# One period of a two-layer decoder's last stage, listed in another order

## The chip, the cores and the metric

The kernel runs on one core of one Trainium2 chip. A core has five engines that each work through a queue of their own, strictly in order: TensorE (PE, matrix products and transposes; its weight loads are shown apart as PEld), VectorE (DVE), ScalarE (ACT), GpSimd (POOL) and SyncE (SP), whose queue here only issues DMAs. Engines wait for one another by semaphores. SBUF is the working memory; PE writes into PSUM, from which ACT and DVE carry the results off.

The metric is the device time of one execution in microseconds (us), the median of several runs. Less is better.

## The reference, cut to what matters

A batch of 16 sequences of 256 tokens of width 128 goes through two layers of attention, cross-attention and a mixture of experts, all in f32. Only the last two steps of the second layer are touched here: a cross-attention whose keys and values come from 64 context rows per sequence (16 heads of 8), and a mixture of 8 experts of which each token uses the best 2.

```
x = x + _L1_xattn_ref(ctx_1024, _layernorm(x, axis=-1), ...)   # softmax over 64 context rows, 16 heads
x = x + _L1_ffn_ref(_layernorm(x, axis=-1), ...)               # router, top 2 of 8, plus a shared expert

# within _L1_ffn_ref
scores = jax.nn.softmax(xt @ gate_w, axis=-1)
top_w, top_i = jax.lax.top_k(scores, TOP_K)
h = jax.nn.silu(jnp.einsum('th,ehi->eti', xt, wg)) * jnp.einsum('th,ehi->eti', xt, wu)
moe = jnp.einsum('eth,te->th', jnp.einsum('eti,eih->eth', h, wd), cw)
```

## The kernel before, in words

The 4096 tokens are 8 chunks (c) of 512 tokens. A chunk has four tiles of 128 tokens (0 to 3) and holds two sequences (0 and 1, of two tiles each). The earlier stages, layer 0 and layer 1's attention, end about 1270 us into the execution; the rest is the stage that is changed. In it the work of one chunk is cut into some 105 parts, and the string PLAN (from L2086) lists all parts once, each with a lag. The program walks the list again and again with a counter c0, and a part with lag n does the work of chunk c0 - n: `fl:1` belongs to the chunk before c0, `S0:-1` to the one after it. So one pass of the list holds the work of four or so chunks at different depths, and the chunks flow through as in a pipeline. The parts are issued under a manual schedule: PE, DVE, ACT and POOL each get their instructions in exactly the order of the list. Parts of chunks 0 and 1 that layer 1's attention already did (`begun`, L1472) are left out.

The parts, by engine (a digit is a tile, a sequence or an expert pair):

- **PE**: S scores of a tile (L1829), T transposes of half a tile's softmax (L1889), P transposes of the softmax's reciprocal sums (L1876), V values (L1907), Y output projection (L1923), xt and xq transposed input and queries (L1440, L1452), ft and fl transposed mixture input and router logits (L1945, L1954), fw the routing weights transposed (L1989), h gate and up products of two experts or of the shared one (L2017, h0 is the shared), d down products of a tile (L2035).
- **DVE**: G row maxima of S (L1836), B scores less maxima (L1840), R sums and reciprocals (L1862, L1863), O and X evacuate V and Y (L1915, L1929), xs and fs statistics (L1422, L1423), fg the router's choice of two experts, twelve small instructions after a copy of fl's result (L1961, L160 to L178), fq its weights (L1972 to L1982), m gate times up (L2024), z the final sum (L2044), D a half tile's transposes carried off (L1898).
- **ACT**: E exponentials (L1848), C the same work as D (L1898), U, xc, xQ, fc and fW carry off P, xt, xq, ft and fw, fn normalises (L1936), fe one exponential for the router (L1966), a the gate's silu (L2021). Exponential and silu come from different tables, so ACT loads a table (ACT_TABLE_LOAD, at the line of the instruction that needs it) whenever the two alternate.
- **POOL**: A two additions that shrink a softmax to a quarter (L1854, L1855), Q spreads R (L1868), K keys (L1464), xb a bias, xr and fr inverse square roots, k multiplies an expert pair by its routing weights (L2030).
- **SP**: fW also writes the routing weights to memory and reads them back spread over all partitions (wrows L1996, spread L2001, 512 KB), for the k parts; z sends two finished tiles to the output (L2051).

Memory that couples the engines: `sx`, one PSUM tile that S writes and G and B read, so that S, G, B take turns; two PSUM buffers ("m") that all of V, xq, Y, T, P, ft, fl, d, xt and fw share in turn, so that each waits for the carrying-off of the one two before it; and one PSUM buffer each for gate and up.

## Time and profile before

| | |
|---|---|
| Median of 3 runs | 1544.63 us (1543.79 to 1545.28) |
| The profiled execution's own time | 1540.27 us |
| Its span, first to last instruction | 1538.6 us |
| Busy over the span | PE 95%, DVE 76%, ACT 63%, POOL 43% |
| The stage that is changed | about 1266 us to the end, 272 us |
| Mean granted TensorE clock over the span | 0.982 |

How to read the views: a page gives busy shares over the whole span, which averages stages with different limits. So the stage has to be read from the timelines of each engine, in which a row is: start in us, duration in us (for a group of several instructions, from the first start to the last end), engine, line, operation, result and operands, shape, count, and in brackets the idle time of the engine before it with the engine and line that ended that idle time. In the table of windows, a row is a stretch, its length, then busy time and number of instructions on PE, PEld, DVE, ACT and POOL, the granted TensorE clock (1.00 is full), the DMA engines' mean busy share and GB/s.

### The profile page before, as it was taken

What the parts mean: (1) busy time and instruction counts of PE and PEld (TensorE: products, weight loads), DVE (VectorE), ACT (ScalarE), POOL (GpSimd) and SP (SyncE); (2) the same over time, 40 slices, a digit from 0 to 9 for tenths busy, and PEclk for the clock granted to TensorE, in tenths of its full rate; (3) what the DMA queues carried; (4) which work ended last, traced back from release to release, by engine and by line L of the source; (5) the groups of instructions that cost most, each with busy time, mean ns of one, the idle gap of its engine ahead of it and who ended that gap; (6) DMA issues with size and microseconds to landing.
All of it is one profiled execution on the core that took longest, in us unless ns stands there. A gap on an engine that the chain in (4) does not pass through costs nothing.

```text
span 1538.6 us, 34876 instructions
## 1 busy us (share of the span) xinstructions
PE 1461.4 (95%) x11569; PEld 1069.0 (69%) x11569; DVE 1175.6 (76%) x4620; ACT 971.1 (63%) x2619; POOL 667.9 (43%) x1102
## 2 busy tenths in 40 slices
PE   7999999999999999899999899999999996899897
PEld 4666666666666666689999777777777764565564
DVE  6666666667676767677878779999999978888863
ACT  5666565656565656354333368888888884767752
POOL 7354646464747464555533311101101015657643
PEclk9999999999999999999999989999999997999999
DMA  7760000000000000457777300000000000122122
GB/s 220 249 202 1 1 14 3 9 8 5 12 1 15 1 15 1 133 172 235 224 237 236 100 22 9 15 15 9 15 1 2 2 1 1 29 53 53 36 62 49
DMA packets 76321, 95.01 MB, mean 62 GB/s; under 512 B 15936, under 2 KB 59200, under 8 KB 76144
## 3 DMA queue, kind: packets, MB, share of 16 engines
q1 hardware_dynamic: 61312, 45.59, 10.9%
q10 hardware_dynamic: 10512, 38.28, 7.7%
q0 software_dynamic: 4320, 8.92, 1.7%
q8 instruction: 94, 1.54, 0.4%
q14 instruction: 83, 0.68, 0.1%
HBM read 64.11 MB, written 28.65 MB: 60 GB/s over the span
## 4 chain that ended last, share of the span: by engine, by line
PE 81%; DVE 12%; ACT 3%; issue 2%; DMA 1%; POOL 0%; POOLq 0%; ACTq 0%; SPq 0%; DVEq 0%
PE t L1659 7%; PE pqk L395 7%; PE s L450 6%; PE o L512 6%; PE t L497 5%; PE s L1627 5%; PE g L1298 4%; PE o L1674 4%; PE y L427 4%; PE y L1316 4%; PE u L1298 4%; PE pv L412 3%; PE pqk L1540 3%; PE yf L2035 2%; PE tx L1889 2%
## 5 line engine op out<-in xcount | busy, mean ns | idle before, releaser
L475 ACT ACTIVATE p<-p,nm 128x128 f32<-128x128 f32 (+1 forms) x512 | 227.5, 446 | 183.9 <-DVE nm L463 174.9
L486 POOL TENSOR_SCALAR p<-p,rs 128x128 f32<-128x128 f32 (+1 forms) x512 | 213.7, 434 | 187.3 <-DVE rs L484 159.4
L1649 ACT ACTIVATE p<-p,nm 128x256 f32<-128x256 f32 x512 | 225.7, 508 | 37.5 <-DVE nm L1638 35.2
L502 DVE COPY pT<-t 128x384 f32<-128x384 f32 x256 | 131.0, 553 | 102.4 <-PE t L497 102.3
L1638 DVE CUSTOM_DVE_ANT_0 p<-s,strip 128x256 f32<-128x256 f32 x512 | 188.1, 419 | 18.3 <-PE s L1627 17.8
L463 DVE CUSTOM_DVE_ANT_0 p<-s,strip 128x128 f32<-128x128 f32 (+1 forms) x512 | 158.1, 346 | 1.3 <-PE s L450 1.3
L1659 PEld LDWEIGHTS t<-ident,p 128*128 128x128 f32 x1024 | 111.2, 142 | 47.4 <-issue 12.6
L1659 PE MATMUL t<-ident,p 128*128 128x128 f32 x1024 | 141.5, 282 | 0.0
L1326 POOL DMA_INDIRECT rows_out<-yr,to x71 | 68.7, 967 | 117.3 <-DVE yr L1325 109.2
L1505 POOL TENSOR_SCALAR ve_a<-mv_a 128x2 f32<-128x2 f32 x16 | 3.7, 231 | 265.0 <-DVE mv_a L1500 264.9
L450 PE MATMUL s<-k,q 64*128 64x128 f32 (+1 forms) x1024 | 118.5, 350 | 0.0
L512 PE MATMUL o<-pT,v 128*64 128x256 f32 (+1 forms) x1024 | 112.8, 340 | 0.8 <-DVE pT L502 0.8
L497 PE MATMUL t<-ident,p 128*128 128x128 f32 x768 | 113.3, 283 | 0.2 <-ACT k L406 0.2
L450 PEld LDWEIGHTS s<-k,q 64*128 64x128 f32 x1024 | 67.0, 186 | 62.5 <-issue 56.3
L512 PEld LDWEIGHTS o<-pT,v 128*64 128x64 f32 x1024 | 62.9, 136 | 61.6 <-issue 25.9
L497 PEld LDWEIGHTS t<-ident,p 128*128 128x128 f32 x768 | 82.1, 141 | 23.2 <-issue 15.4
L475 ACT ACTIVATION_READ_ACCUMULATOR p<-p,nm 128x1 f32 x512 | 96.5, 188 | 0.0
L1306 ACT ACTIVATE gs<-gs 128x512 f32<-128x512 f32 x71 | 44.7, 630 | 77.0 <-DVE gs L1305 64.9
L1667 DVE COPY pT<-t 128x512 f32<-128x512 f32 x128 | 88.1, 688 | 6.2 <-PE t L1659 3.2
L1627 PE MATMUL s<-k,q 32*128 32x256 f32 x1024 | 85.3, 408 | 0.6 <-DVE nm L1638 0.5
L421 DVE COPY v<-pv 128x512 f32<-128x512 f32 x64 | 44.0, 687 | 50.8 <-PE pv L412 50.8
L790 POOL DMA_INDIRECT rows_in<-xn,slot_in x64 | 64.2, 1004 | 33.8 <-DVE nm L463 20.5
(338 smaller groups left out, 3487.8 us busy)
## 6 DMA issues: line engine op xcount, KB each, us to landing
gu<-in_L_ffn_gate_up_w ACTq DMA_DIRECT2D x71, 512.0 KB
rows_in<-zero SPq DMA_DIRECT2D x131, 130.0 KB
spread<-wrows SPq DMA_DIRECT2D x16, 512.0 KB
xr<-rows_in SPq DMA_DIRECT2D x71, 65.0 KB
y<-rows_out SPq DMA_DIRECT2D x16, 256.0 KB
x<-in_x SPq DMA_DIRECT2D x8, 256.0 KB
out_x<-yo SPq DMA_DIRECT2D x16, 128.0 KB
rows_out<-yr,to POOLq DMA_INDIRECT x71, 3.7
```

The source lines that it names most:

```text
L450: nc.tensor.matmul(ps_of[b, h][:, cols], q[rows, u2, iq], k[rows, u2, 0:nk], start=True, stop=True,)
L463: nc.vector.tensor_tensor_reduce(out=pr[:, cols], in0=ps[:, cols], in1=strip[:, h, P : 2 * P] if it == 0 else strip[:, h, :], scale=1.0, s ...
L475: nc.scalar.activation(pr[:, cols], pr[:, cols], AF.Exp, bias=nm[:, it : it + 1], scale=-1.0, accum_out=sm[:, it : it + 1],)
L486: nc.gpsimd.tensor_scalar(pr[:, cols], pr[:, cols], rs[:, it : it + 1], 1.0, ALU.mult, ALU.mult)
L497: nc.tensor.transpose(ps[:, cols], pr[:, cols], ident)
L502: nc.vector.tensor_copy(pT_of[b, h], tp_of.pop((b, h)))
L512: nc.tensor.matmul(po[rows, c0:N], v[:, jt, h % 8 * DH : (h % 8 + 1) * DH], pT[:, 0:N] if jt == 0 else pT[:, N:], start=(jt == 0), stop=(j ...
L1298: nc.tensor.matmul(ps[:, f, :], gu[:, lo + f * P : lo + (f + 1) * P], xT, start=True, stop=True,)
L1627: nc.tensor.matmul(ps_of[b, h][:, it, :], q[rows, g, it * P : (it + 1) * P], k[rows, g, :], start=True, stop=True,)
L1638: nc.vector.tensor_tensor_reduce(out=pr[:, it, :], in0=ps[:, it, :], in1=strip1[:, h, (1 - it) * P : (1 - it) * P + N], scale=1.0, scalar= ...
L1649: nc.scalar.activation(pr[:, it, :], pr[:, it, :], AF.Exp, bias=nm[:, it : it + 1], scale=-1.0)
L1659: nc.tensor.transpose(ps[:, jt, it * P : (it + 1) * P], pr[:, it, jt * P : (jt + 1) * P], ident,)
```

## The change

Only the string PLAN is replaced. The same functions are called for the same chunks, with two exceptions: the part D30 (DVE) becomes C30 (ACT), and the lags are numbered anew since the list now begins at another part. The lists hold 105 parts each.

```
         PLAN = (
-            "h3:2 Q1:0 a3:2 T21:0 B3:0 T11:0 K1:-1 m3:2 R2:0 xs0:-2 C21:0 S0:-1 T10:0 xr:-1 "
-            "C11:0 h4:2 P0:0 k1:2 k2:2 C10:0 V0:0 G0:-1 B0:-1 fn:1 a4:2 U0:0 ft:1 m4:2 fc:1 "
-            "O0:0 xs1:-2 E3:0 S1:-1 k3:2 Y0:0 G1:-1 fl:1 h0:1 k4:2 X0:0 d0:2 fg:1 T20:0 z0:2 "
-            "E0:-1 B1:-1 d3:2 C20:0 fs0:0 z3:2 d2:2 xt:-2 S2:-1 A3:0 fe:1 a0:1 fq:1 z2:2 "
-            "Q2:0 A0:-1 R3:0 Q3:0 fw:1 xc:-2 G2:-1 d1:2 z1:2 m0:1 fW:1 E1:-1 T31:0 K0:-3 "
-            "C31:0 T30:0 h1:1 P1:0 B2:-1 E2:-1 U1:0 S3:-1 A1:-1 D30:0 a1:1 V1:0 R0:-1 A2:-1 "
-            "xq:-2 xb:-2 G3:-1 O1:0 xQ:-2 m1:1 Y1:0 h2:1 a2:1 T00:-1 R1:-1 C00:-1 X1:0 fs1:0 "
-            "T01:-1 fr:0 Q0:-1 C01:-1 m2:1 "
+            "A0:0 a1:2 fs0:1 V1:1 z1:3 O1:1 xq:-1 xs0:-1 S3:0 K0:-2 R0:0 Y1:1 m1:2 xQ:-1 X1:1 "
+            "T21:0 fs1:1 C21:0 A1:0 h2:2 T10:0 G3:0 Q0:0 a2:2 xb:-1 m2:2 T11:0 fr:1 C10:0 h3:2 "
+            "T00:0 C11:0 T01:0 B3:0 k2:2 a3:2 C00:0 S0:-1 R1:0 m3:2 k1:2 xr:-1 xs1:-2 C01:0 "
+            "T20:0 fn:1 G0:-1 C20:0 Q1:0 A2:0 h4:2 a4:2 k3:2 B0:-1 m4:2 P0:0 V0:0 U0:0 O0:0 "
+            "k4:2 ft:1 S1:-1 Y0:0 fc:1 fl:1 R2:0 h0:1 G1:-1 a0:1 X0:0 Q2:0 d3:2 fg:1 z3:2 E3:0 "
+            "T30:0 fe:1 B1:-1 A3:0 C30:0 d0:2 E0:-1 xt:-2 m0:1 z0:2 S2:-1 fq:1 xc:-2 R3:0 Q3:0 "
+            "T31:0 d2:2 C31:0 fw:1 G2:-1 z2:2 h1:1 E1:-1 P1:0 K1:-2 fW:1 U1:0 d1:2 B2:-1 E2:-1 "
         )
```

For one period the queues then read as follows, from the router's logits on.

| Queue | Before | After |
|---|---|---|
| PE | fl h0 d0 T20 d3 d2 xt S2 fw d1 T31 T30 h1 P1 S3 V1 xq Y1 h2 ... | fl h0 d3 T30 d0 xt S2 T31 d2 fw h1 P1 d1 V1 xq S3 Y1 T21 h2 ... |
| DVE | G1 X0 fg z0 B1 fs0 z3 fq z2 ... | R2 G1 X0 fg z3 B1 m0 z0 fq R3 G2 z2 B2 ... |
| ACT | fc E3 E0 C20 fe a0 xc fW E1 C31 E2 U1 a1 ... | fc a0 E3 fe C30 E0 xc C31 E1 fW U1 E2 a1 ... |
| POOL | k3 k4 A3 Q2 A0 Q3 K0 A1 A2 ... | Q1 A2 k3 k4 Q2 A3 Q3 K1 A0 K0 A1 ... |
| SP | output of z2 and z3, wrows, output of z1 and z0, spread | output of z2 and z3, wrows, spread, output of z1 and z0 |

## The prediction

> **What bounds the stage now.** First the table of windows over the stage: five periods, from the h2 part of the first chunk to that of the sixth, take 147.38 us (29.5 each), and PE is busy in all but 11.4 of them. Then PE's own waits in that stretch: 10.7 of the 11.4 us have one cause.

> ```profile
> 1327.12:1474.50 147.38, 135.93 (x945) 89.18 (x944) 128.53 (x317) 102.99 (x154) 97.08 (x123) 0.98 0.19 45
> ...
> PE yf L2035 <- DVE yo L2044: 10.7, 5, 2.6
> ```

> Once a period PE waits until DVE has carried off a down product. PE's timeline of one period shows where, and DVE's and POOL's show why.

> ```profile
> 1398.00 0.96 PE L1954 MATMUL lg<-rw,xTf 128*128 128x8 f32 x8
> 1398.81 1.10 PE L2017 MATMUL g<-xTf,sg 128*128 128x512 f32 x2
> ...
> 1401.73 0.60 PE L1889 MATMUL tx<-ident,px 128*128 128x128 f32 x4
> 1404.14 0.49 PE L2035 MATMUL yf<-sd,hb 128*128 128x128 f32 x2 [1.82 <-DVE yo L2044]
> ```
> ```profile
> 1400.24 1.12 DVE L169 TENSOR_TENSOR eq_f<-eq_f,mi_f 128x32 f32<-128x32 f32 x1
> ...
> 1402.85 0.97 DVE L169 TENSOR_TENSOR eq_f<-eq_f,mi_f 128x32 f32<-128x32 f32 x1
> ...
> 1508.76 0.19 DVE L169 TENSOR_TENSOR eq_f<-eq_f,mi_f 128x32 f32<-128x32 f32 x1
> ```
> ```profile
> 1400.04 1.28 POOL L1854 TENSOR_TENSOR half<-px 128x512 f32<-128x512 f32 x1 [1.40 <-ACT px L1848]
> ...
> 1402.51 1.25 POOL L1854 TENSOR_TENSOR half<-px 128x512 f32<-128x512 f32 x1
> ```

> PE issues fl at 1398.00, then h0, d0, T20, and stands before d3, whose PSUM buffer is d0's and is free only after z0; on DVE z0 stands behind fg. fg runs 1399.13 to 1403.81, 4.7 us. Two of its instructions take 1.12 and 0.97 us: each has both inputs in SBUF and ends when POOL's addition (A3, then A0) does. In the drain, with POOL idle, the same instruction takes 0.19 and fg 2.7 us (1507.64 to 1510.36). So 2.0 us of fg is waiting for POOL; in other periods (1428 to 1433) it is 2.7.

> The gap has a second price. In one-microsecond windows the granted clock falls to half after the gap of 1373 (2.59 us) and after that of 1462 (1.82 us), and not after the other three.

> ```profile
> 1374.00:1375.00 1.00, 1.00 (x5) 1.00 (x6) 1.00 (x2) 1.00 (x1) 0.00 (x0) 0.50 0.00 0
> ...
> 1404.00:1405.00 1.00, 0.86 (x7) 0.86 (x8) 1.00 (x2) 0.98 (x2) 0.58 (x1) 1.00 0.00 0
> ```

> About 3.4 us run at half clock each time, which costs 1.7. A period with neither extra (V1 at 1384.28 to V1 at 1412.93) takes 28.65, of which 26.8 is PE's work and small waits.

> **The change, part by part.** No instruction is added or removed but for two table loads and D30; the sum is about places.

> *Removed: the router's collision.* POOL after: A2, k3, k4, Q2, then A3 only after E3. I walk one new period on all four queues, T=0 at fl's issue, with the durations of the rows (issue to issue on PE: S 0.65, T 0.44, h 1.72, h0 1.80, d 1.12, V 1.0, xq 0.95; G and B 1.14 each; E 1.05; A 2.04; k 1.24). G1 ends at 0.75, X0 at 1.1; fg starts there, as before (1.13 after fl). POOL has done A2 at -1.5, k3 at -0.3 and k4 at 0.95, before fg's first two-input instruction at 1.5. So fg takes 2.7 and ends at 3.85, z3 at 4.1. Before, z0 ended 6.1 after fl. If POOL is late by a microsecond, k4 delays fg by under one, which the next wait hides.

> *Added: a wait for E3.* Its place in ACT's queue is now behind a0. a0 needs h0's gate (0.81+1.10=1.91) and ends at 2.55; the table load follows it.

> ```profile
> 1397.52 1.28 ACT L1848 ACT_TABLE_LOAD   x1
> 1398.81 2.19 ACT L1848 ACTIVATE px<-px,rstd_x 128x1024 f32<-128x1024 f32 x2
> ```

> The exponential starts 1.29 after the load does: E3 runs 3.85 to 5.0. T30 transposes E3's result and stands on PE before d0, so PE, done with d3 at 3.89, waits to 5.05: **1.16 us, in place of 1.82 to 2.6**. Queued behind T30: d0, xt, S2, T31, d2, fw, h1. Behind E3 on ACT: fe, C30, E0, xc; fe at 5.0 is still ahead of fq, which now stands behind z0 (7.0).

> [...]

> *Further round the period.* d0 5.5, xt 6.6, S2 7.15 (B1 done 5.3), T31 7.8, d2 8.25, fw 9.4 (fq done 8.2), h1 9.8, P1 11.5, d1 11.85 (fW has freed the buffer at 10.6), V1 12.95, xq 13.95, S3 14.9 (B2 done 11.2), Y1 15.55, T21 16.0, h2 16.4. The silu load stands behind E2, so a1 comes only at 14.5 to 15.1 and m1 at 16.3; h2 needs a1 at 16.4 and m1 at 17.3: held. Then T10, T11 18.15, h3 19.05, T00, T01 20.75, S0 21.65 (B3 done 20.3), T20, h4 22.75, P0 24.45, V0 24.8, ft 25.8, S1, Y0, and fl at 27.55. With the odd tenths that PE loses at PSUM turns in the old period (0.35) that is 27.9; the other way, 28.65-1.82+1.16, is 28.0. ACT loses two of its four loads a period (-2.57) and gains C30 (+0.48); DVE loses D30 (-0.60): neither sets the end, so nothing is counted.

> *Moved past queues.* On SP, z1's output now comes after the spread instead of before it: neutral. The spread itself loses cover. k2 wants it at 19.45, where before k1 came 14 us after the weights were ready. The chain that ended last shows its length when POOL waited for it:

> ```profile
> 1514.21 1.46 DMA wrows<-cTf
> 1516.36 6.83 DMA spread<-wrows
> 1523.35 1.26 POOL hb L2030
> ```

> From the copy's end (1514.19) to k1 is 9.15 us. After fW at 10.6 that gives 19.75. k2, k1, xr and Q1 follow in POOL's queue (4.2 us), so P0 can start at 24.0; PE asks at 24.45. A2 behind Q1 ends at 26.0, R2 wants it at 26.15. Cover left: 0.2 to 0.45 us. I count 0.

> *The sum.* Five periods: 147.4 - 10.7 + 5 x 1.16 = 142.5. Of the half-clock stretches (2 x 1.7) I take half back, the trace showing no gap as short as 1.16 to judge by: 140.8, so -6.6. [...] Before the first of these periods: the turns of S, G and B through `sx` (3.8 each at 1275 to 1300) are as many in both orders; fg of the first chunk loses its 1.4 of collision (1311.56 to 1315.78 is 4.2), and half of its half-clock stretch (1319 to 1323) is 0.8: -2. The next-to-last period (25.10) loses its waits on z and gains E3's: -0.4. The drain is one chain, router, spread, weighting, down, in both: -0.2. In all **-9.2**: span 1538.6 to 1529.4, its own time 1540.27 to 1531.1. The median of the runs shown lies 4.36 above that execution; the same difference gives **1535.5**.

> **The rivals.** Less than 0.2% (3.1 us) either way is what a measurement of this kernel can't tell from no change.

> - *As summed* (-5 to -14, that is 1531 to 1540): 0.55. Its range holds the clock going either way and 0.5 us per period of waits unseen.
> - *The gap closes*: E3 is let through early enough or PE's other parts fill it. Then 5 x 1.16 more and no half clock at all: -17, 1528. For it: ACT has 2 us a period more room. Against it: the order of a0, load, E3, T30 is fixed. 0.07.
> - [...] 0.15, half of it beyond 3.1.
> - *The change does nothing to the wait*: POOL is so late in every period that k3 and k4 fall into fg as A3 and A0 did. Then z3 ends at 6.1 and the gap is the old one: 1545. 0.08.
> - *Slower: the spread lands late.* Place: k2, with k1, xr, Q1, A2 behind it in POOL's queue, P0 on PE behind Q1, fg behind R2. Six periods, each microsecond of landing past 0.45 of cover adds one to each. The gain of 9.2 is eaten from 9.15+0.45+1.5 = 11.1 us after fW on; at 12 it is 5 slower, 1550. For it: the cover falls from 14 us to 9, and outputs share the queue. Against it: in four periods DMA traffic after fW ends 8 us later, each time within half a microsecond. 0.15.

> Range: 1527 to 1547 leaves out the far half of the last and little else, some 0.13. Faster: 0.55+0.07+0.08=0.70 and 0.03 of the last case; same: 0.07+0.06+0.02; slower the rest, 0.12; I round to 0.73, 0.13, 0.14.

> **What would show it.** Right: PE's wait for yo L2044 in the stage falls from five gaps of about 2 us to none or under 0.3; a new wait of PE tx L1889 on ACT px L1848 of 1.0 to 1.3 us once a period; ACT_TABLE_LOAD twice a period, one at L1848 and one at L2021; L169 at 0.19 to 0.4 in the middle periods; h2 starts 27.7 to 28.3 apart. Wrong: POOL hb L2030 waiting on spread in more than the last chunk; PE rt L1876 waiting on POOL rs; half-clock windows after gaps of 1.2; a wait of PE for DVE's m parts, which the walk gives 0.1 to 1 us of room.

## The result, and the profile after

The new list takes 1530.89 us (median of 6 runs, 1529.08 to 1532.58) where the kernel before, over 6 runs, takes 1544.87 (1543.68 to 1545.68): 0.991 of it, 95% interval 0.9898 to 0.9923, or 14.0 us less. The two profiled executions lie 10.4 us apart (1540.27 and 1529.89). Predicted were 9.2 us for the execution and 1535.5 for the median, with 1531 to 1540 as the case "as summed": the median lies at its lower edge.

The table of windows of the new kernel, from the h2 of the first chunk to that of the second, and from there to that of the seventh (columns as in the row of before: length, then busy time on PE, PEld, DVE, ACT and POOL, the granted clock, the DMA engines' share and GB/s):

```profile
1325.42:1354.13 28.71, 26.99 (x192) 17.47 (x191) 23.30 (x65) 18.56 (x30) 18.97 (x26) 1.00 0.22 54
1354.13:1489.35 135.22, 128.46 (x905) 84.34 (x903) 106.46 (x296) 87.68 (x143) 89.03 (x112) 1.00 0.20 48
```

By the starts of h2 the periods are 28.71, 27.96, 27.95, 27.96, 26.50 and 24.85. The first five, which took 147.5 us before, take 139.1: 8.5 us less, at full clock throughout. PE's waits over the stage (in all, times, longest), and then POOL's:

```profile
PE tx L1889 <- ACT px L1848: 9.3, 7, 2.3
```
```profile
POOL hb L2030 <- DMA spread<-wrows: 16.0, 3, 14.9
```

PE's waits for yo L2044, 10.7 us before, are gone, and in their place stands T30's wait for E3's px. POOL waits for the spread routing weights 14.9 us in the last chunk, and 1.1 us in two others together.

One period of the new kernel by engine: PE, then DVE, ACT and POOL (start, duration, line, operation, and in brackets the idle time before it and what ended it).

```profile
1393.31 0.96 PE L1954 MATMUL lg<-rw,xTf 128*128 128x8 f32 x8
...
1396.15 1.06 PE L2035 MATMUL yf<-wd,hb 128*128 128x128 f32 x8
1398.38 0.66 PE L1889 MATMUL tx<-ident,px 128*128 128x128 f32 x4 [1.18 <-ACT px L1848]
```
```profile
1395.48 0.19 DVE L169 TENSOR_TENSOR eq_f<-eq_f,mi_f 128x32 f32<-128x32 f32 x1
...
1396.83 0.19 DVE L169 TENSOR_TENSOR eq_f<-eq_f,mi_f 128x32 f32<-128x32 f32 x1
...
1397.24 0.29 DVE L2044 TENSOR_TENSOR yo<-x,yf 128x128 f32<-128x128 f32 x1
```
```profile
1395.27 0.60 ACT L2021 ACTIVATE gs<-g 128x512 f32<-128x512 f32 x1 [2.46 <-PE g L2017]
1395.88 1.28 ACT L1848 ACT_TABLE_LOAD   x1
1397.18 1.15 ACT L1848 ACTIVATE px<-px,rstd_x 128x1024 f32<-128x1024 f32 x1
```
```profile
1398.40 1.28 POOL L1854 TENSOR_TENSOR half<-px 128x512 f32<-128x512 f32 x1 [3.99 <-ACT px L1848]
```

POOL idles 4 us before A3, so the two-input instructions of the router's choice take 0.19 us in place of about 1; fg takes 2.7, z3 starts 3.9 us after fl. PE then waits 1.18 us for E3, which comes straight behind a0 and a table load of 1.28. Over the stage ACT loads tables 17 times, not 27.

**Where the 10.5 us of the span came from**, by the starts of h2 in both traces: 0.8 are there already when the stage begins, 0.8 come before the first h2, 8.5 in the five periods, 0.25 in the next one and 0.25 in the drain.

### The profile page after: what moved, and what is told of

The parts are those of the page before. It is cut to its first block, busy times and chain, and to the rows that moved or that the text cites. A ratio compares the mean times of both kernels' runs of the same rounds, so it can differ in the third digit from the quotient of the medians.

```text
span 1528.1 us, 34888 instructions
## 1 busy us (share of the span) xinstructions
PE 1457.1 (95%) x11569; PEld 1065.8 (70%) x11569; DVE 1160.5 (76%) x4612; ACT 961.2 (63%) x2617; POOL 665.6 (44%) x1102
## 3 DMA queue, kind: packets, MB, share of 16 engines
HBM read 64.11 MB, written 28.65 MB: 61 GB/s over the span
## 4 chain that ended last, share of the span: by engine, by line
PE 82%; DVE 10%; ACT 3%; issue 2%; POOL 2%; DMA 1%; POOLq 0%; SPq 0%; ACTq 0%; DVEq 0%
PE t L1659 7%; PE pqk L395 7%; PE s L450 6%; PE o L512 6%; PE t L497 6%; PE s L1627 5%; PE g L1298 4%; PE o L1674 4%; PE y L427 4%; PE y L1316 4%; PE u L1298 4%; PE pv L412 3%; PE pqk L1540 3%; PE g L2017 2%; PE yf L2035 2%; DVE p L1638 2%
## 5 line engine op out<-in xcount | busy, mean ns | idle before, releaser
L486 POOL TENSOR_SCALAR p<-p,rs 128x128 f32<-128x128 f32 (+1 forms) x512 | 212.3, 431 | 188.1 <-DVE rs L484 160.1
```

The costliest lines, as they stand in the source:

```text
L486: nc.gpsimd.tensor_scalar(pr[:, cols], pr[:, cols], rs[:, it : it + 1], 1.0, ALU.mult, ALU.mult)
```

## The experiments

Twelve runs, one of them the new list again (e5), were meant to tell four things apart: whether the collision with POOL was the cost, what of POOL's work does it, what the idle time of PE costs beyond itself, and whether the 1.18 us that remain can be had. The first four ran on one chip and the next four on another, where both kernels take some 20 us longer, nearly all of it ahead of the stage (S0 starts at 1288.8 to 1291.5 us, not at 1265 to 1267); e10 to e12 ran on a third and e13 on a fourth. So a kernel is compared by its ratio to the kernel before on its own chip, and by the stage's length from the first S0 to the end of the span in its profile, which is 262.8 and 262.9 us for the new list on two chips.

| Kernel | Median, us | Before there | Ratio (95%) | Stage, us | Middle period, us | Half-clock stretches in the middle periods |
|---|---|---|---|---|---|---|
| before | 1544.87 | | 1 | 272.5 | 28.65 to 31.1 | 2 |
| new list | 1530.89 | 1544.87 | 0.991 (0.9898 to 0.9923) | 262.8 | 27.95 | 0 |
| e1_act_order | 1557.03 | 1565.67 | 0.9943 (0.9925 to 0.9962) | 264.8 | 28.07 | 0 |
| e2_collide | 1567.03 | 1565.67 | 0.9998 (0.9981 to 1.0016) | 280.7 | 30.7 | 4 |
| e3_gap | 1572.22 | 1565.67 | 1.0043 (1.0024 to 1.0062) | 280.0 | 30.7 | 5 |
| e4_d0_first | 1553.03 | 1565.67 | 0.991 (0.989 to 0.9931) | 260.5 | 27.74 | 0 |
| e5_after | 1553.61 | 1569.15 | 0.9908 (0.9892 to 0.9924) | 262.9 | 27.95 | 0 |
| e6_fill | 1555.06 | 1569.15 | 0.992 (0.9899 to 0.9941) | 263.3 | 27.95 | 0 |
| e7_half_gap | 1557.40 | 1569.15 | 0.993 (0.9911 to 0.9948) | 266.2 | 28.45 | 0 |
| e9_d0_z0 | 1551.13 | 1569.15 | 0.9891 (0.9872 to 0.9909) | 260.2 | 27.73 | 0 |
| e10_s2_first | 1530.25 | 1545.93 | 0.9908 (0.989 to 0.9926) | 260.4 | 27.64 | 0 |
| e11_split | 1550.81 | 1545.93 | 1.0043 (1.0026 to 1.0059) | 283.2 | 30.7 | 2 |
| e12_gap2 | 1544.41 | 1545.93 | 0.9991 (0.9982 to 1.0) | 276.0 | 28.8 or 30.35 | 4 |
| e13_split2 | 1535.53 | 1547.69 | 0.9924 (0.9901 to 0.9946) | 267.7 | 28.77 | 0 |

The middle period is from fl to fl; the stretches are counted from the first h2 on. Added operations write a tile that nothing reads. Two profiled executions are far from their medians: that of the kernel before took 4.4 to 4.6 us less, that of e2 took 6.2 us more.

### One part of the change alone: ACT's order

The old list with five ACT parts in another order: a0 goes first, as in the new list, and E0 last. The table loads fall from 27 to 17 with it.

```
 ACT behind fc
-E3 E0 C20 fe a0 ...
+a0 E3 C20 fe E0 ...
```

> The old list with five ACT parts in another order and nothing else: a0, E3, C20, fe, E0 after fc, where it was E3, E0, C20, fe, a0. Theory (the gain is the router's choice no longer meeting POOL's additions, since E3 and so A3 come later): fg takes 2.7 to 2.9 us in the middle periods, where it took 4.2 to 5.5; PE's wait for z0 falls from 1.8 to 2.6 to about 0.3; d2 waits 0.1 for C20 and fw about 0.4 for fq, which now touches A3's second addition. Net 1.2 us a period and the half-clock stretches gone: 8 to 14 us below the kernel before, 1531 to 1537. Rival (the gain lies in the other moves of the list: d3 ahead, T31 apart, V ahead of S3, D30 to ACT): at most 2 us below, 1543 to 1545.

Of the 9.7 us that the stage loses with the whole list, this part alone takes 7.7 in the profiles, and by the ratios (0.9943 and 0.991) some six tenths of the gain: with E3 behind a0, A3 and A0 come later, and fg is left alone. But the collision isn't gone, it has moved. DVE and PE of one period, and POOL's two additions:

```profile
1394.96 0.19 DVE L169 TENSOR_TENSOR eq_f<-eq_f,mi_f 128x32 f32<-128x32 f32 x1
...
1399.02 1.19 DVE L1982 TENSOR_TENSOR comb<-eq_f,eq_f 128x32 f32<-128x32 f32 x1
```
```profile
1400.47 0.60 PE L1989 MATMUL cT<-ident,comb 128*8 128x128 f32 x4 [1.11 <-DVE yo L2044]
```
```profile
1396.45 1.29 POOL L1854 TENSOR_TENSOR half<-px 128x512 f32<-128x512 f32 x1 [4.68 <-ACT px L1848]
...
1398.90 1.26 POOL L1854 TENSOR_TENSOR half<-px 128x512 f32<-128x512 f32 x1
```

Now fq's last instruction, which also has two inputs in SBUF, takes 1.19 us and ends within a tenth of a microsecond of A0, and fw (cT) waits 1.1 us. cT's PSUM buffer comes free with a yo, and that yo stands behind comb on DVE: it starts at 1400.14, and would have started about 1.0 earlier behind a comb of 0.19. The period is 28.07 with this gap in place of 27.95 with the other. The rest of the new order is worth the last 2 us of the stage in the profiles, about 5 by the ratios, give or take 3.

### Is it the collision, and what of POOL's work makes it?

The new list with work on POOL put back where the additions stood: three additions of 128x512 (e2), or seven fills of the same tile (e6), behind Q2.

```
+        pad = hbp.tile([P, 4, P], F32, tag="pad", name="pad", bufs=1)
+        def busy(c):
+            for _ in range(3):                                   # e2
+                nc.gpsimd.tensor_tensor(pad, ones.unsqueeze(1).to_broadcast([P, 4, P]),
+                    ones.unsqueeze(1).to_broadcast([P, 4, P]), ALU.add)
+            for _ in range(7): nc.gpsimd.memset(pad, 1.0)        # e6
-            ... X0:0 Q2:0 d3:2 fg:1 ...
+            ... X0:0 Q2:0 w:1 d3:2 fg:1 ...
```

> The new list with three additions of 128x512 on POOL (about 1.28 us each, into a tile that nothing reads) behind Q2, where POOL stands idle for 4 us until A3: they start with fg and are over before A3 can start. Theory (a DVE instruction with two inputs in SBUF stands while POOL's addition runs): fg grows from 2.7 to between 4.5 and 6 us, z3 ends at 6 to 7 us after fl's issue instead of 4.2, PE's d0, which ran at 5.5, waits for it by 0.5 to 1.5 us, so 4 to 12 us slower than the new kernel: 1535 to 1543. Rival (the gain has another cause, and POOL's idle time is free): no change from the new kernel, 1530 to 1532.

> The new list with seven fills of 128x512 on POOL behind Q2, into a tile that nothing reads: about as long as the three additions that gave back the whole gain (3.3 to 3.9 us, from 0.95 us for a fill of 128x1024), but instructions that read nothing. Theory (what holds up the router's instructions with two inputs in SBUF is POOL reading SBUF): fg stays 2.7 us, the gap before T30 stays 1.18, the time is that of the new list within 0.2%. Rival (POOL being busy, or being late with what follows, is enough): fg 4 us or more and a wait of PE for z3 or z0, 10 us or more above the new list.

POOL and DVE of one period with the additions, then with the fills:

```profile
1425.12 3.28 POOL L2094 TENSOR_TENSOR pad<-ones 128x512 f32<-128x512 f32 x3
...
1427.58 0.86 DVE L169 TENSOR_TENSOR eq_f<-eq_f,mi_f 128x32 f32<-128x32 f32 x1
...
1429.60 0.93 DVE L169 TENSOR_TENSOR eq_f<-eq_f,mi_f 128x32 f32<-128x32 f32 x1
```
```profile
1419.44 4.03 POOL L2094 MEMSET pad<- 128x512 f32 x7
...
1420.56 0.19 DVE L169 TENSOR_TENSOR eq_f<-eq_f,mi_f 128x32 f32<-128x32 f32 x1
...
1421.90 0.19 DVE L169 TENSOR_TENSOR eq_f<-eq_f,mi_f 128x32 f32<-128x32 f32 x1
```

The additions give back the whole gain (0.9998), some 14 us and not the 4 to 12 that were expected: fg takes 5.3 to 6.3 us from the second chunk on (its second long instruction above runs into A3, which starts at 1429.15), d0 waits 0.9 to 1.8 us for z3, on top of T30's 1.18, and four half-clock stretches follow. The fills are longer (4.03 us) and cover all of fg, and fg isn't touched; the time is within 0.1% of the new list's on that chip, and A3, a little late behind them, costs nothing. So POOL being busy or late was not the cause.

What is left is what the additions do and the fills don't, and that is to read SBUF; no run here parts this from other differences between the two. Two more things fit it. In the earlier layers of the kernel before, nb_f (L363, 128x4, two inputs in SBUF) takes 0.32 to 0.35 us and ends with POOL's operation in five of the six cases where it meets a multiplication of one tile by a column (L486); in the sixth, which falls between two of these, and in the two others it takes 0.15. And the hb product (L2024), whose second input is in PSUM, is not held up in the kernel before: it takes 0.69 us where it lies wholly beside POOL's k (seven of its 40 cases) and 0.67 to 0.69 in the others. In the rows of e2 and e6 the router's instruction with two inputs in SBUF takes 0.86 and 0.93 us beside additions, and 0.19 beside fills.

### What the idle time costs

The new list with ACT copies of 128x512 between a0 and E3, so that PE's one gap, before T30, grows: two copies (e3), one (e7), one and a copy of 128x128 (e12).

```
-            ... a0:1 X0:0 ... E3:0
+            ... a0:1 w:1 X0:0 ... E3:0      # w: 2, 1, or 1 and a quarter copies on ACT
```

> The new list with two copies of 128x512 on ACT (about 0.5 us each, into a tile that nothing reads) between a0 and E3: E3 ends 1.0 us later, and PE's gap before T30 grows from 1.18 to about 2.15 us, as long as the old kernel's gaps. Theory that a gap of this length sets off stretches of half clock: one to three of six middle gaps are followed by about 3.4 us at a granted clock of 0.50, 1.7 us each; 6.5 us for the gaps and 2 to 5 for the clock, 8 to 12 us slower than the new kernel: 1539 to 1543, mean granted clock down by 0.001 to 0.003. Rival (the half-clock stretches have nothing to do with the gap): 6 to 7 us slower, 1537 to 1538, clock as in the new kernel.

> The new list with one copy of 128x512 on ACT between a0 and E3 (two gave a gap of 2.32 us and 20 us more). Expected gap before T30: 1.18 + 0.57 = 1.75. If the granted clock only depends on the length of the idle time and 1.75 is still short enough: 0.57 us a period, 4 us above the new list. If 1.75 is enough to drop it after each gap, as 2.32 was: 0.57 + 1.6 a period, about 15 above. In between, as in the kernel before, where two gaps in five of 1.8 to 2.6 did it: 7 to 10 above.

> The new list with a copy of 128x512 and one of 128x128 on ACT between a0 and E3. Expected gap before T30: 1.18 + 0.57 + 0.25 = 2.0 us, just past the 1.8 of idle in one window of 3.41 us from which the clock seems to fall. Theory: a half-clock stretch follows where at least 1.82 us of the gap lie in one window, and none where the gap straddles two, which of the two is a matter of the phase: 2 to 5 stretches in the seven periods, 9 to 16 us above the new list. Rival (the length of the gap alone decides, with its limit between 1.75 and 2.32): all or none, about 6 or about 18 above.

The gaps came out at 2.32, 1.67 and 2.00 us, against 1.18 (2.15, 1.75 and 2.0 were expected). By its gap alone e3's period would grow by 1.14 us, and it grew by 2.75, because a stretch of 3.41 us at half clock follows each of the five middle gaps, where one to three were expected; the kernel lost some 20 us and not 8 to 12. With one copy the period grows by 0.50, the kernel by 3.8 us, and no stretch appears. What decides is not the length of the gap alone. The half-clock stretches of all the traces are whole multiples of 3.413 us (one cut off by the end of a trace aside) and, within a trace, begin on one grid of 3.413 (in the stage of the kernel before at 1319.30, 1373.91 and 1462.66 us, 16 and 26 times 3.413 apart). The table of windows, cut on that grid, first for the kernel with the gap of 2.00 us:

```profile
1374.07:1377.49 3.42, 1.42 (x13) 1.38 (x13) 2.02 (x3) 2.76 (x5) 1.28 (x1) 1.00 0.00 0
1377.49:1380.90 3.41, 3.41 (x20) 2.43 (x19) 2.37 (x10) 1.54 (x2) 1.45 (x3) 0.50 0.00 0
1404.79:1408.21 3.42, 1.75 (x16) 1.75 (x17) 1.73 (x2) 2.76 (x5) 1.65 (x2) 1.00 0.00 0
1408.21:1411.62 3.41, 3.41 (x32) 2.69 (x31) 3.21 (x12) 2.77 (x5) 1.74 (x4) 1.00 0.00 0
```

In the first row the whole gap lies in one window: PE is idle 3.42 - 1.42 = 2.00 us, and the next window runs at 0.50. In the third the same gap lies across an edge, 1.67 us on this side, and the next window keeps 1.00. Of this kernel's six gaps of 2.00 us four lie whole in a window and are followed by a stretch (the period is 30.35), two don't and aren't (28.78), so a stretch costs 1.6 us here. By the ratios the kernel lies 12.5 us above the new list, in the range that the theory gave and at neither of the rival's values.

In the kernel before, the same cut explains which gaps were followed by half clock and which were not:

```profile
1370.50:1373.91 3.41, 0.82 (x8) 0.58 (x7) 3.24 (x9) 0.83 (x3) 2.91 (x4) 1.00 0.00 0
1373.91:1377.33 3.42, 3.42 (x16) 3.42 (x17) 2.65 (x11) 1.84 (x2) 0.00 (x0) 0.50 0.00 0
1428.52:1431.94 3.42, 2.46 (x17) 1.74 (x15) 3.21 (x7) 1.72 (x3) 3.17 (x4) 1.00 0.00 0
1431.94:1435.35 3.41, 1.78 (x16) 1.78 (x16) 3.27 (x10) 1.97 (x3) 1.18 (x2) 1.00 0.00 0
1435.35:1438.76 3.41, 3.41 (x35) 2.84 (x34) 2.98 (x12) 1.73 (x4) 0.41 (x1) 1.00 0.14 41
```

Of its two gaps of 2.6 us, the one at 1371 lies in one window (2.59 idle) and is followed by half clock; that at 1431 is split into 0.96 and 1.63 and is not. And the three gaps of 1.82 are at the limit: one was followed by a stretch, one was not, and the third lay across an edge.

That the window counts, and not the single gap, is seen in e2, where T30's gap of 1.18 and d0's of 0.9 to 1.1 together leave PE idle for 1.86 to 1.93 us of one window, and four times half clock follows:

```profile
1396.41:1399.82 3.41, 1.55 (x13) 1.12 (x11) 3.20 (x9) 2.01 (x2) 2.68 (x3) 1.00 0.00 0
1399.83:1403.24 3.41, 3.20 (x14) 2.96 (x14) 2.47 (x7) 1.72 (x3) 0.73 (x1) 0.50 0.00 0
```

The other way to idle as much, at two places, was tried with copies ahead of a1: five (e11), then two (e13).

```
-            "A0:0 a1:2 ...
+            "A0:0 w:2 a1:2 ...
```

> The new list with five copies of 128x512 on ACT ahead of a1, so that h2 waits for its gate buffer some 1.2 us, more than 20 us away from T30's gap of 1.18: about the same idle time of PE in a period (2.3 to 2.6 us) as the one gap of 2.32 that cost 30.7 us a period. Theory (the granted clock is judged in windows of 3.41 us, each by PE's idle time in it alone, and falls for the next one only from about 1.8 us of idle): no stretch at half clock in the middle periods, the period grows by the second gap alone to 29.0 to 29.5, 7 to 11 us above the new list. Rival (what counts is PE's idle share over a longer time): a half-clock stretch in nearly every period, 30.5 or more, 18 us or more above.

> The new list with two copies of 128x512 on ACT ahead of a1 in place of the five, which gave a second gap of 2.54 us before T21, twice what was meant. With three copies of 0.51 less: a gap of 1.0 to 1.1 before T21, 24 us away from the one of 1.18 before T30. The same two copies between a0 and E3 made one gap of 2.32 and cost 2.75 us a period (20 us in all). Theory (idle time is judged within one window of 3.41 us): no stretch at half clock in the middle periods, 28.9 to 29.2 us a period, 7 to 9 us above the new list. Rival (PE's idle share over a period or more counts): half-clock stretches as there, 30.5 a period and 18 us or more above.

Both missed their size. In e11 not h2's gate buffer was waited for but xQ, which stands behind a1 on ACT: a second gap of 2.54 us before T21, so the period is 30.7 without a half-clock stretch (28.0 and 2.7), and the first expectation of the time is wrong: the kernel lies some 20 us above the new list, which is the rival's number without its cause. It still tells the two apart: PE idles 3.7 us a period, more than the 2.3 of e3, and of its four gaps of 2.54 only the first was followed by a stretch (the other stretch in the table follows a wait of 3.72 us in the first period); the idle share of a period is not what counts. But it doesn't bear out a limit of 1.8: of the first gap 1.92 us fell into one window, of the other three 1.96 to 1.97, and these kept full clock. In e13 the second gap was 0.6, not 1.0, and the kernel lies some 2 us above the new list by the ratios (5 by the stage), not 7 to 9; the same two copies that cost 2.75 us a period in front of E3 cost 0.82 here and no stretch, but its idle time, 1.78 in all, would be under the limit in one window too, so it adds nothing on that question.

### The 1.18 us that are left

The new list with d0 ahead of T30 on PE (e4); with z0 listed ahead of xt as well (e9); with S2 ahead of xt as well (e10). The new list itself ran beside e9 (e5).

```
-  PE  ... d3 T30 d0 xt S2 T31 d2 ...
+  PE  ... d3 d0 T30 xt S2 T31 d2 ...        # e4, e9
+  PE  ... d3 d0 T30 S2 xt T31 d2 ...        # e10
+  list ... xt:-2 z0:2 m0:1 ...               # e4
-  list ... A3:0 C30:0 E0:-1 xt:-2 m0:1 z0:2 ...
+  list ... z0:2 A3:0 C30:0 E0:-1 xt:-2 m0:1 ...        # e9, e10
```

> The new list with d0 ahead of T30 on PE and z0 ahead of m0 on DVE. d0's PSUM buffer is the router logits', free at fg's first instruction, so PE can run d0 while it would stand waiting for E3: d3 ends at 3.7 us after fl's issue, d0 at 4.85, T30 then waits 0.2 instead of 1.18. Theory (that one gap is what is left of PE's idle time in a period): 0.8 to 1.0 us a period over six or seven periods, 5 to 7 us faster than the new kernel: 1524 to 1526. Rival (another wait takes its place at once: xt for z0, which stands behind B1, or S2 for B1): less than 2 us gained, 1529 to 1531.

> The new list itself, as the reference for its variants on this chip. Expected: 0.991 of the kernel before, five middle T30 gaps of 1.18 us, no stretch at half clock in the middle periods.

> The new list with d0 ahead of T30 as in the earlier experiment, and z0 listed ahead of xt, so that xt can take d0's PSUM buffer instead of waiting for C30. Theory (1.16 us a period was lost to E3's chain, and parts that are ready can fill it): no gap before T30, none before xt, period 27.95 less 0.7 to 1.2, so 5 to 8 us below the new list. Rival (the period has another bound close by, the spread that lands with 0.2 to 0.45 us of cover): POOL waits for spread or PE for rs, the period stays above 27.6 and the time within 2 us of the new list.

> The list of the previous experiment with S2 ahead of xt on PE. There xt got T30's PSUM buffer again and waited 0.68 us for C30 although d0's was free. S2 is ready (B1 is done) and fills 0.65 of it; d2, one place further on, then needs xt's buffer and may wait up to 0.4 us for xc. Expected: the wait before xt below 0.1, a wait of d2 of 0 to 0.4, so 0.2 to 0.6 us a period and 1.5 to 4 us less than the previous experiment (0.989 of the kernel before). Rival: the 0.68 only moves on to d2 or T31, no change.

PE of e9 in one period:

```profile
1395.28 1.06 PE L2035 MATMUL yf<-wd,hb 128*128 128x128 f32 x8
1396.40 0.66 PE L1889 MATMUL tx<-ident,px 128*128 128x128 f32 x4
1397.73 0.66 PE L1440 MATMUL tpx<-ident,x 128*128 128x128 f32 x4 [0.68 <-ACT pTx L1898]
```

T30 no longer waits, but xt does: 0.68 us for C30, in e4 and in e9 alike. The PSUM buffer that xt got was thus T30's, although d0's was free earlier (in e9 z0 ends at 1396.88 and C30 at 1397.67); listing z0 ahead of xt didn't change that. The theories of e4 and e9 failed, and e4's rival, that another wait takes the gap's place at once, held: the period went from 27.95 to 27.73, not by 0.7 to 1.2. With S2 in the gap (e10) the wait moved on to d2, 0.43 us for xc, as far as had been feared, and the period is 27.64; 0.1 us a period, where 0.2 to 0.6 were expected. All three take the stage down by 2.3 to 2.7 us in the profile, but the times (ratios 0.991, 0.9891, 0.9908, with intervals of 0.002 to either side) can't be told from the new list's own 0.9908. No version measurably better than the new list was found.

## Why the prediction was right, and where it was off

**What bounded the kernel: shown.** The prediction put fg's 2.0 us of excess down to POOL's A3 and A0. With POOL idle there fg takes 2.7 and PE's waits for yo are gone; with additions put back the gain is gone; with fills it stays.

**The new wait: shown, and of the right size.** T30's gap was predicted at 1.16 us and is 1.17 to 1.18 in every middle period. The walk put z3 at 4.1, d0 at 5.5, xt at 6.6, S2 at 7.15, T31 at 7.8 and d2 at 8.25 after fl; in the trace d0 starts at 5.56, xt at 6.68, S2 at 7.21, T31 at 7.85 and d2 at 8.35. The period was to be 27.9 to 28.0 and is 27.95.

**The table load: as the row showed.** The load takes 1.28 us, and E3 starts 1.29 or 1.30 after the load did in all seven chunks of the new list that have one there, in series on the path that sets the end. The prediction's 0.15 (0.08 and 0.07 in its sums) stands for an E3 that comes about a microsecond later than that; no middle period of the new list shows such a delay, with T30's gaps at the 1.17 to 1.18 above.

**The half clock: the term that was mis-sized.** Half of the 3.4 us in five periods was taken back; all of it came back. The prediction went by the length of the gaps; the shorter of the two that it saw half clock follow was one of 1.82 us. What the traces show is windows of 3.41 us on a grid that doesn't move with the gaps, and between 1320 and 1520 us half clock followed seven of the ten windows with 1.82 to 2.0 us of idle time and all 21 with 2.0 and more. A lone gap of 1.18 stays under that wherever it falls, and none of the 18 in three traces of the new list (e5 and e6 included) was followed by a stretch. But the short gap alone doesn't explain it. The prediction said that no gap as short as 1.16 was there to judge by; the trace of before has one, of 1.20 us, at the start of the stage, and half clock follows it (the idle time of its window is 1.24 in all):

```profile
1268.09:1271.50 3.41, 2.17 (x15) 1.26 (x11) 2.13 (x5) 0.37 (x1) 0.00 (x0) 1.00 0.00 0
1271.51:1274.92 3.41, 1.70 (x5) 1.11 (x5) 1.09 (x2) 0.37 (x1) 0.00 (x0) 0.50 0.00 0
```

What sets that window apart from those of the periods stays open. In the five periods -6.6 was predicted and -8.5 measured: about 1.7 of the difference is this term.

**The head: too large.** -2 was predicted before the first h2, -0.8 is what came within the stage: the collision in the first fg does go (1.5 us by the rows, not 1.4), but the first chunk's half-clock stretch is there after too (at 1315, behind a wait of T30 for E3 of 2.29 us), and there are small waits: P's rt L1876 for POOL's rs, 0.83 us before the first h2 and 0.54 in the first period, which takes 28.71 in place of 27.95, and T21's 0.62 before the first h2. The wait for rs is a sign that the prediction had named as one against it; it doesn't come again. Another 0.8 was there when the stage began, which the change doesn't explain. The two errors, -1.9 and +1.2, and this 0.8 make up most of the step from -9.2 to -10.5.

**From the execution to the median: a step that didn't hold.** The prediction added the 4.36 us by which before's median lay over its profiled execution. For the new kernel that difference is 1.0. So the medians fell 14 where the executions fell 10.4, and the median came out 4.6 us below the one predicted, in the range but not by this step. The runs offer a cause, which is not shown: the kernel before has gaps at and above the limit, so the number of its half-clock stretches may change from execution to execution, and each costs 1.6 to 1.7 us. Over the executions of the kernel before on three chips (27, 9 and 30) the time rises 1.4, 1.7 and 1.3 us for each 0.001 of mean clock lost (correlations -0.86, -0.82 and -0.71); a stretch at half clock would make 1.5 by an estimate from its 3.41 us and a span of 1540 (1.7 us, and 0.0011 of the clock). Its profiled execution would then have been one with some two or three stretches fewer than the median's. Against it: if so, the runs of the kernel before should differ more than those of the new list, whose gaps start none, and of the six of each, those of the kernel before lie within 2.0 us and those of the new list within 3.5.

**The edits counted at nothing.** D30's move to ACT was not tried alone, and the two table loads fewer only together with ACT's order (e1); nothing in the trace after shows ACT or DVE at a point that sets the end. The spread landed as the row of the drain said: the copy ends at 1376.02, its DMA traffic at about 1384.5, and k2 began at 1385.24, right behind fr; in two middle chunks POOL waited for it, 0.44 and 0.66 us, which the prediction had named as a sign against it. The rival that this would be late didn't come about, as PE doesn't wait for rs there, but the cover was as thin as said.

**The other rivals.** That the gap closes: no, the order fixes it, and e4, e9 and e10 show that closing it by hand gives 0.2 to 0.3 us a period, as the next PSUM turn takes its place. That POOL would be late enough to collide all the same: no, POOL idles 4 us there.

## What to carry to other kernels

When a chain of small two-input DVE instructions stands on the path, look at what POOL reads at the same time: with POOL's large additions a few microseconds later this chain took 2.7 us in place of 4.7, and fills in their place did it no harm. Before a gap of the bounding TensorE is priced, look at how much idle time falls into one window of the granted clock, other gaps in that window included: in these periods, with windows of 3.41 us, lone gaps of up to 1.67 us (e7) cost only their length, while 2.0 us or more in one window cost another 1.6. And carry a prediction from a profiled execution to a median with care: the two lay 4.4 us apart for one list and 1.0 for the other.

## What the runs showed of the hardware

| Idle time of PE in a window | Windows | Next window at half clock |
|---|---|---|
| under 1.5 us | 777 | 3 |
| 1.5 to 1.82 | 11 | 1 |
| 1.82 to under 2.0 | 10 | 7 |
| 2.0 and more | 21 | 21 |

The three in the first row ran at half clock themselves, two in the drain and one in the head; the one in the second row, at 1.50 us, is a window of two gaps in the head. Between 1.82 and 2.0 the three that kept full clock are those of e11, at 1.96 and 1.97, and just past 1520 e3 has one at 1.89 that kept it too, so the limit is known to no better than 0.15 us: matmul ends are modelled.

Ahead of that part the limit does not hold: at the start of the stage, between 1266 and 1306 us, eleven of the fourteen traces have a window at full clock with only 1.2 to 1.5 us of idle time that half clock follows. Nor is the stage's place on the grid all chance: its first S0 starts 0.2 to 1.6 us behind an edge in all fourteen traces. No run here tells why.

A period near 30.72 us, which is nine windows, keeps its gaps at the same place in their windows. e3 and e2 came out there with their idle time whole in a window, and paid for a stretch in nearly every period; e11 came out there with its gap of 2.54 us across an edge (0.57 and 1.96 to 1.97), and after the first paid for none.
